# A selective state-space layer with gated experts in fp32: matmuls on zeros at the start, and one exponential moved from VectorE to GpSimd

## The chip, the cores and the metric

The kernel runs on one core of a Trainium2 chip. The metric is the device time of one execution in microseconds (us); the time of a kernel is the median of its runs. A profiled execution gives the span from its first to its last instruction and a trace of what every engine did. The engines are TensorE (PE in the profile, its weight loads PEld), VectorE (DVE), ScalarE (ACT), GpSimd (POOL) and the queues that issue DMAs (SP, and those of ACT and POOL).

## The reference

`x` has 64 sequences (b), 64 heads (h) and 1024 positions (l), all fp32. Each head has a convolution kernel over the positions, made of 64 complex modes, and the result goes through a layer of 64 experts of rank 16, of which each token takes 16:

```python
dt = exp(log_dt);  A = -exp(log_A_real) + 1j * A_imag;  dtA = A * dt[:, None]
Cs = C * (exp(dtA) - 1) / A
K  = 2 * einsum('hn,hnl->hl', Cs, exp(dtA[:, :, None] * arange(L))).real
y  = causal_conv(x * mask, K) + x * mask * D[:, None]      # then * mask; mask = l < length[b]
scores = y @ Wr.T;  gates = softmax of the 16 largest scores, zero elsewhere
h   = einsum('nd,krd->nkr', y, A_experts)
out = x + 2 * einsum('nkr,kdr->nd', h * gates[:, :, None], B_experts)
```

The part that the change touches is `Cs`, the factor of each mode. With dtA = u + iv it needs exp(u) - 1, the sine of v and 1 - cos v, and a division by A. The kernel forms exp(u) itself as s * (1 + q): s is a power of two, q a polynomial of degree eight, so that exp(u) - 1 = s q + (s - 1).

## The kernel before

**Staging.** The heads are worked in 8 groups of 8 heads (512 tokens). For each group, tables of the modes' powers give a Toeplitz block (`toep`) and two factors (`bt`, `w`) of a chunked convolution: TensorE forms the states of each chunk (`pu`, L652), VectorE carries them from chunk to chunk (L664 to L670), and TensorE adds the part inside a chunk (`pc`, L681) and the part across (L690). Then come the scores (L760) and the first expert product (L585), which is a seven-product scheme for 2x2 blocks. The second expert product (L1083) is in the last third of the span and uses a two-level scheme of the same kind.

**The start.** Everything waits for the parameters of the modes. `par_sb` (log dt, log of -A's real part, A's imaginary part, C) is the first load on SP. VectorE forms dt and the real part of A by `exp_parts` (L413) on 128x64, then `dt_re` = u (`p_dtre`, L449) and `theta` = v, and the angle in turns in two parts (`tu_hi`, `tu_lo`; L454 to L464). Then several chains run:

- `tables(0)` (L240), the wide tables of the first group on 128x516: magnitude by ScalarE (L252), angle by VectorE (L253 to L264), sines by ScalarE (L267 to L270), and the two multiplies into `w` (L273, L275);
- `real_part` (L470): a second `exp_parts` on `dt_re`, 128x32, and `em1` = exp(u) - 1;
- `angle` (L477): the sines of the modes' angles, `s2`, and the reciprocal of |A|^2 (`rden`);
- `products` (L515): the factors `alpha`, `beta` and their negatives.

`together` (L401) takes one step of each chain in turn. These instructions are issued on VectorE in the order in which they are written (`first_order`, L435, a manual schedule), and so are ScalarE's up to L551 (`first_copies`). In `products`, `e_im` (L517) is the first that uses `em1`; the first `w` multiply follows it. With `alpha` and the others, VectorE makes `b` (L350 to L354), TensorE turns it (`pb`, L337), ScalarE copies it (`bt`, L339), and `pu` follows.

**The sums of the expert weights.** The seven-product scheme needs sums of quarters of the weight matrix `at`. The quarters arrive on SP (L165). TensorE forms two of the sums by multiplying each addend with the identity into one bank (`factors_by_identity`, L187): four banks, three addends each, 128x512. ScalarE copies the banks out (`s1` at L200, `s2` at L204); the first of these copies is in ScalarE's order before the sines, the other seven after them and before `bt`. GpSimd waits for the last x tile of the group (`behind_landing`, L206) and then issues DMAs that add the other sums (L214, L223).

**The order on TensorE** is set by the planner of the framework, from its own costs and the order of writing, save for instructions named in `keep_in_program_order`, which keep their order among themselves. `ps_c` holds two PSUM banks, used later by `pc`.

Of the kernel before, what the change touches and what calls it, by code (L numbers as in the profile page):

```python
# [37 lines left out]
F32 = mybir.dt.float32  # L38
I32 = mybir.dt.int32
AF = mybir.ActivationFunctionType  # L40
ALU = mybir.AluOpType
# [3 lines left out]
P = 128  # L45
NB = 64
NH = 64
L = 1024
# [14 lines left out]
NP = NH // 2  # L63
# [29 lines left out]
def body(ctx: ExitStack, tc, x, xo, lens, par, dvec, dgrp, at, bm, wt, cst, out):  # L93
    nc = tc.nc
    V = nc.vector
    G = nc.gpsimd
# [4 lines left out]
    def pool(stack, name, bufs, side, **kw):  # L101
        return stack.enter_context(tc.tile_pool(name=name, bufs=bufs, side=side, **kw))
# [4 lines left out]
    ps_c = psum.enter_context(tc.tile_pool(name="ps_c", bufs=2, space=PSUM))  # L107
# [15 lines left out]
    prep = pool(prep_ctx, "prep", 1, "right")  # L123
# [13 lines left out]
    ident = cst_sb[:, NW : NW + P]  # L137
# [16 lines left out]
    def factor(wpool, name, t):  # L154
        return wpool.tile([P, KH, L // 2], F32, tag=t, name=f"{name}{t}")
# [31 lines left out]
    def factors_by_identity(a21, a22, a11, a12, out):  # L187


        s1, s2, s4 = (factor(wp, "wa", t) for t in ("s1", "s2", "s4"))  # L190
        out.extend((a11, a12, s4, a22, s1, s2, a21))
        banks = [ps_f.tile([P, L // 2], F32, tag="pf", name=f"sum_{k}") for k in range(KH)]

        def add(bank, a, first=False, last=False):
            nc.tensor.matmul(bank, lhsT=ident, rhs=a, start=first, stop=last, skip_group_check=True)

        for k in range(KH):
            add(banks[k], a21[:, k, :], first=True)
            add(banks[k], a22[:, k, :])
            nc.scalar.copy(s1[:, k, :], banks[k])  # L200
            yield
        for k in range(KH):
            add(banks[k], a11[:, k, :], last=True)
            nc.scalar.copy(s2[:, k, :], banks[k])  # L204
            yield
# [176 lines left out]
    def new(name, w=NP, dtype=F32, keep=False):  # L382
        pool = const if keep else prep
        return pool.tile([P, w], dtype, tag=f"p_{name}", name=f"p_{name}")

    def tt(o, a, b, o_):
        V.tensor_tensor(out=o, in0=a, in1=b, op=o_)  # L387
        return o

    def ts(o, a, s1, o1, s2=None, o2=None):  # L390
        if o2 is None:
            V.tensor_scalar(out=o, in0=a, scalar1=s1, scalar2=None, op0=o1)
        else:
            V.tensor_scalar(out=o, in0=a, scalar1=s1, scalar2=s2, op0=o1, op1=o2)
        return o

    def stt(o, a, s, o1, b, o2):
        V.scalar_tensor_tensor(out=o, in0=a, scalar=s, in1=b, op0=o1, op1=o2)  # L398
        return o

    def together(*chains):  # L401

        chains = list(chains)
        while chains:
            for c in list(chains):
                if next(c, chains) is chains:
                    chains.remove(c)

    def some(it, n):
        for _ in range(n):  # L410
            yield next(it, None)

    def exp_parts(xin, name, w, out):  # L413

        xc = ts(new(name + "x", w), xin, -87.0, ALU.max, 88.0, ALU.min)
        k = ts(new(name + "k", w), xc, LOG2E, ALU.mult)
        yield
        ts(k, k, MAGIC, ALU.add, MAGIC, ALU.subtract)
        yield
        stt(xc, k, -LN2_HI, ALU.mult, xc, ALU.add)  # L420
        yield
        stt(xc, k, -LN2_LO, ALU.mult, xc, ALU.add)
        s = new(name + "s", w, I32)
        ts(s, k, 127.0, ALU.add, 8388608.0, ALU.mult)
        yield
        q = ts(new(name + "q", w), xc, 1.0 / math.factorial(8), ALU.mult)
        for i in range(7, 0, -1):
            yield
            stt(q, q, 1.0 / math.factorial(i), ALU.add, xc, ALU.mult)
        out += [s.bitcast(F32), q]  # L430
# [5 lines left out]
    first_order.enter_context(tc.manual_schedule(engines={V.engine}))  # L436
    first_copies = ExitStack()
    first_copies.enter_context(tc.manual_schedule(engines={nc.scalar.engine}))
    log_both = par_sb[:, 0:2, :].rearrange("p a h -> p (a h)")
    a_im, c_re, c_im = (par_sb[:, i, :] for i in (2, 3, 4))  # L440
    parts = []
    together(exp_parts(log_both, "e", 2 * NP, parts))
    s, q = parts
    both = new("both", 2 * NP)
# [3 lines left out]
    a_re = ts(new("are"), both[:, NP:], -1.0, ALU.mult)  # L448
    dt_re = tt(new("dtre", keep=True), a_re, dt, ALU.mult)  # L449
    theta = tt(new("theta"), a_im, dt, ALU.mult)  # L450

    hi, lo, t1 = new("hi"), new("lo"), new("t1")
# [14 lines left out]
    parts = []  # L467
    em1, r, sin, s2, den, rden = (new(n) for n in ("em1", "r", "sin", "s2", "den", "rden"))

    def real_part():  # L470
        yield from exp_parts(dt_re, "f", NP, parts)
        yield
        tt(em1, parts[0], parts[1], ALU.mult)
        yield
        stt(em1, parts[0], -1.0, ALU.add, em1, ALU.add)

    def angle():  # L477
        ts(r, turns, MAGIC, ALU.add, MAGIC, ALU.subtract)
        yield
        tt(r, tu_hi, r, ALU.subtract)  # L480
        yield
        tt(r, r, tu_lo, ALU.add)
        yield
        ts(r, r, HALF_IN, ALU.min, -HALF_IN, ALU.max)
        nc.scalar.activation(sin, r, AF.Sin, scale=2.0 * math.pi)
        nc.scalar.activation(s2, r, AF.Sin, scale=math.pi)
        yield
        tt(den, a_re, a_re, ALU.mult)
        yield
        tt(t1, a_im, a_im, ALU.mult)  # L490
        yield
        tt(den, den, t1, ALU.add)
        yield
        V.reciprocal(rden, den)
        yield
        tt(s2, s2, s2, ALU.mult)
        yield
        ts(s2, s2, 2.0, ALU.mult)

    wa, wb = [], []  # L500
    marks = {}
    sums = factors_by_identity(*wa_quarters, wa)
    steps0 = tables(0)
    next(steps0)
    for _ in some(sums, 1):
        pass
    together(some(steps0, 5), real_part(), angle())

    e_im = new("eim")
    e_re = new("ere")  # L510
    n_re, n_im, t2 = new("nre"), new("nim"), new("t2")
    alpha, nbeta, nalpha = (new(n, keep=True) for n in ("alpha", "nbeta", "nalpha"))
    beta = new("beta")

    def products():  # L515
        ts(e_re, s2, -1.0, ALU.mult, 1.0, ALU.add)
        stt(e_im, em1, 1.0, ALU.add, sin, ALU.mult)  # L517
        yield
        tt(e_re, e_re, em1, ALU.mult)
        tt(t1, e_im, a_im, ALU.mult)  # L520
        tt(n_im, e_im, a_re, ALU.mult)
        yield
        tt(e_re, e_re, s2, ALU.subtract)
        yield
        tt(n_re, e_re, a_re, ALU.mult)
        tt(t2, e_re, a_im, ALU.mult)
        yield
        tt(n_re, n_re, t1, ALU.add)
        tt(n_im, n_im, t2, ALU.subtract)
        yield  # L530
        tt(n_re, n_re, rden, ALU.mult)
        tt(n_im, n_im, rden, ALU.mult)
        yield
        tt(alpha, c_re, n_re, ALU.mult)
        tt(t1, c_im, n_im, ALU.mult)
        tt(beta, c_re, n_im, ALU.mult)
        tt(t2, c_im, n_re, ALU.mult)
        yield
        tt(alpha, alpha, t1, ALU.subtract)
        tt(beta, beta, t2, ALU.add)  # L540
        yield
        ts(alpha, alpha, 2.0, ALU.mult)
        ts(nbeta, beta, -2.0, ALU.mult)
        ts(nalpha, alpha, -1.0, ALU.mult)

    together(products(), some(steps0, 2))
    scales.update(alpha=alpha, nbeta=nbeta, nalpha=nalpha)

# [591 lines left out]
    def steps_of(g):  # L1140
        return tables(g) if g < NG else iter(())
# [14 lines left out]
    y = got.pop()  # L1156
    spread = {}
    products, done = counted(first(0, y, spread)), [0]
    ahead(products, 1)
    for _ in steps:  # L1160
        pass
    ahead(products, 1)
    for g in range(NG):
# [18 lines left out]
        if g == 0:  # L1182
            tables1, n = steps_of(1), 0
# [50 lines left out]
    n = 0  # L1234
    for _ in products:
# [3 lines left out]
        if n in (5, 6):  # L1239
            i = (1, 6)[n - 5]  # L1240
# [18 lines left out]
    def lpool(name, bufs):  # L1259
        return pool(ctx, name, bufs, "left")  # L1260

    tp2 = lpool("tp2", 1)
    op = [lpool(f"op{i}", 4) for i in range(3)]
# [55 lines left out]
```

## Time and profile before

| | |
|---|---|
| Time, median of 3 runs | 961.89 us (961.85 to 961.9) |
| Profiled execution | 961.78 us |
| Its span | 960.0 us |
| Mean granted TensorE clock | 1.000 |
| TensorE busy | 948.8 us, 99% of the span |
| VectorE busy | 729.1 us, 76% |
| GpSimd busy | 332.5 us, 35% |
| ScalarE busy | 152.4 us, 16% |

How to read it: the page gives busy time by engine, the chain of work that ended last, and groups of instructions. A line of a group has the source line, the engine, the operation, output and inputs with their shapes and count, then total busy time and the mean in ns, then the idle time of the engine just before them and what ended it. A line of the timeline has the start in us from the span's beginning, the duration in us, the engine, the line and the instruction; in brackets is the idle time before it and what released it. Names in the trace carry a prefix: `p_em` is `em1`, `p_eim` is `e_im`, `was` and `waa` are the quarters and sums of the weights (the tiles' common beginnings), `sum` is one of the four banks.

The start in short: the first instruction of VectorE after `par_sb` has landed is at 3.22 us, the first matmul at 4.14 us, the first `pb` at 19.79 us and the first `pu` at 21.76 us.

### The profile page before, as it was taken

What the parts mean: (1) busy time and instruction counts of PE and PEld (TensorE: products, weight loads), DVE (VectorE), ACT (ScalarE), POOL (GpSimd) and SP (SyncE); (2) the same over time, 40 slices, a digit from 0 to 9 for tenths busy, and PEclk for the clock granted to TensorE, in tenths of its full rate; (3) what the DMA queues carried; (4) which work ended last, traced back from release to release, by engine and by line L of the source; (5) the groups of instructions that cost most, each with busy time, mean ns of one, the idle gap of its engine ahead of it and who ended that gap; (6) DMA issues with size and microseconds to landing.
All of it is one profiled execution on the core that took longest, in us unless ns stands there. A gap on an engine that the chain in (4) does not pass through costs nothing.

```text
span 960.0 us, 11875 instructions
## 1 busy us (share of the span) xinstructions
PE 948.8 (99%) x4259; PEld 723.4 (75%) x4259; DVE 729.1 (76%) x1697; ACT 152.4 (16%) x302; POOL 332.5 (35%) x285
## 2 busy tenths in 40 slices
PE   7999999999999999999999999999999999999998
PEld 2476676676676676676686588888888888888887
DVE  8899899597687687687577589878956875786674
ACT  5345051311410320220101000000000000000000
POOL 0212212051051051051041022248645654854565
PEclk9999999999999999999999999999999999999999
DMA  8916244162262252244341273662683476268332
GB/s 285 231 42 183 100 129 150 45 182 87 91 190 77 88 176 94 88 134 121 102 137 57 78 259 129 247 258 78 219 307 98 165 241 208 77 220 289 116 115 104
DMA packets 68985, 143.97 MB, mean 150 GB/s; under 512 B 9472, under 2 KB 20288, under 8 KB 68928
## 3 DMA queue, kind: packets, MB, share of 16 engines
q1 hardware_dynamic: 49420, 94.40, 29.2%
q0 software_dynamic: 16864, 47.22, 15.6%
q10 hardware_dynamic: 2644, 1.61, 0.6%
q8 instruction: 33, 0.54, 0.2%
q14 instruction: 24, 0.20, 0.1%
HBM read 94.89 MB, written 47.25 MB: 148 GB/s over the span
## 4 chain that ended last, share of the span: by engine, by line
PE 97%; DVE 2%; DMA 0%; issue 0%; ACT 0%; DVEq 0%
PE h L585 41%; PE s L1083 35%; PE pc L681 6%; PE pc L690 5%; PE pu L652 5%; PE psh L760 3%; PE pb L337 1%; PE psc L770 0%; PE last L1083 0%; DMA par_sb<-in_par 0%; DVE ey L918 0%; DVE p_eq L398 0%; DVE y L698 0%; DVE f L387 0%; DVE w L387 0%
## 5 line engine op out<-in xcount | busy, mean ns | idle before, releaser
L398 DVE SCALAR_TENSOR_TENSOR s<-s,turn 128x128 f32<-128x128 f32 (+1 forms) x558 | 154.2, 325 | 21.0 <-ACT s L657 15.6
L585 PE MATMUL h<-y,waa 128*128 128x256 f32 x512 | 119.4, 382 | 0.0
L585 PE MATMUL h<-y,was 128*128 128x256 f32 x512 | 117.1, 381 | 0.0
L585 PE MATMUL h<-ty,was 128*128 128x256 f32 x512 | 116.1, 379 | 0.0
L585 PEld LDWEIGHTS h<-y,waa 128*128 128x128 f32 x512 | 95.1, 190 | 23.9 <-issue 7.6
L585 PEld LDWEIGHTS h<-y,was 128*128 128x128 f32 x512 | 96.2, 190 | 19.1 <-issue 5.7
L585 PEld LDWEIGHTS h<-ty,was 128*128 128x128 f32 x512 | 97.0, 190 | 14.6 <-issue 1.5
L845 POOL TENSOR_TENSOR hg<-h_p,gx 128x512 f32<-128x512 f32 x16 | 27.6, 1727 | 221.2 <-DVE h_p L398 217.2
L845 POOL TENSOR_TENSOR hg<-h_u,gx 128x512 f32<-128x512 f32 x32 | 47.7, 1491 | 100.7 <-DVE h_u L387 96.5
L698 DVE TENSOR_TENSOR y<-pc,mask 128x512 f32<-128x512 f32 x64 | 41.2, 683 | 45.1 <-PE pc L690 45.1
L1097 ACT COPY p<-s 128x512 f32<-128x512 f32 x28 | 16.4, 585 | 312.4 <-PE s L1083 312.4
L942 POOL TENSOR_TENSOR o<-o,acc_a 128x512 f32<-128x512 f32 x32 | 47.7, 1509 | 41.4 <-ACT acc_a L960 21.6
L818 POOL DMA_DIRECT2D gx<-gt_dram x56 | 34.1, 624 | 73.9 <-DMA gt_dram<-gt 73.8
L681 PE MATMUL pc<-x,toep 128*128 128x512 f32 x128 | 58.9, 594 | 0.0
L585 PE MATMUL h<-ty,waa 128*128 128x256 f32 x256 | 58.4, 381 | 0.0
L657 ACT COPY s<-pu 128x448 f32<-128x448 f32 x62 | 32.7, 531 | 157.0 <-PE pu L652 157.0
L585 PEld LDWEIGHTS h<-ty,waa 128*128 128x128 f32 x256 | 48.2, 190 | 9.9 <-issue 3.5
L652 PE MATMUL pu<-x,bt 128*64 128x448 f32 x256 | 53.4, 549 | 0.0
L690 PE MATMUL pc<-s,w 64*128 64x448 f32 x248 | 52.8, 555 | 0.0
L942 POOL TENSOR_TENSOR o<-o,b_room 128x512 f32<-128x512 f32 x32 | 49.1, 1556 | 9.8 <-DVE b_room L387 9.8
L387 DVE TENSOR_TENSOR o<-o,s 128x512 f32<-128x512 f32 x50 | 34.1, 681 | 23.0 <-PE s L1083 17.3
L387 DVE TENSOR_TENSOR hg<-hg 128x512 f32<-128x512 f32 x64 | 43.0, 684 | 9.2 <-POOL hg L845 8.5
(238 smaller groups left out, 1570.1 us busy)
## 6 DMA issues: line engine op xcount, KB each, us to landing
x<-in_x SPq DMA_DIRECT2D x32, 512.0 KB
hg_dram<-hg POOLq DMA_DIRECT2D x16, 1024.0 KB, 5.8
o<-in_xo SPq DMA_DIRECT2D x64, 256.0 KB
out<-o SPq DMA_DIRECT2D x63, 256.0 KB
gx<-gt_dram POOLq DMA_DIRECT2D x56, 256.0 KB, 5.4
qy<-hg_dram SPq DMA_DIRECT2D x28, 512.0 KB
r<-hg_dram SPq DMA_DIRECT2D x26, 512.0 KB
hg_dram<-hg POOLq DMA_DIRECT2D x16, 768.0 KB, 4.9
```

Of the source, the lines that this page charges most:

```text
L387: V.tensor_tensor(out=o, in0=a, in1=b, op=o_)
L398: V.scalar_tensor_tensor(out=o, in0=a, scalar=s, in1=b, op0=o1, op1=o2)
L585: nc.tensor.matmul(bank[:, ii, :], lhsT=fac[n - 1][:, k, (j + ii) * P : (j + ii + 1) * P], rhs=rf[n - 1][:, k, :], start=(first and ii == ...
L652: nc.tensor.matmul(pu[hh * NS : (hh + 1) * NS, :], lhsT=bt[:, i, (1 - c) * P + hh * NS : (1 - c) * P + (hh + 1) * NS], rhs=xt[:, hh, : NCH ...
L657: marks["s"] = nc.scalar.copy(s[:, c], pu.rearrange("p (k b) -> p k b", b=NB))
L681: nc.tensor.matmul(pc, lhsT=toep[:, 2 * i + hh, :], rhs=xt[:, hh, :], start=True, stop=False)
L690: m = nc.tensor.matmul(pcs[hh][:, NB:], lhsT=w[o : o + NS, c, i, 1:], rhs=s[o : o + NS, c].rearrange("p k b -> p (k b)"), start=False, sto ...
L698: marks["y"] = V.tensor_tensor(out=y[:, :, i // 2, 2 * (i % 2) + hh, :], in0=pcs[hh].rearrange("p (k b) -> p k b", b=NB), in1=mask, op=ALU ...
L818: i = queue.dma_start(gx[:, ii, :], gt_dram[g, c * n : (c + 1) * n, :].unsqueeze(1).to_broadcast([n, RANK, TOK]),)
L845: G.tensor_tensor(out=o, in0=a, in1=b, op=op)
L942: tc.keep_in_program_order(G.tensor_tensor(out=o, in0=a, in1=b, op=op_))
L1083: nc.tensor.matmul(bank[:, ii, :], lhsT=left_[i - 1][:, k, ii * P : (ii + 1) * P], rhs=right_[i - 1][:, k, :], start=(first and ii == rows ...
```

## The change

There are three edits.

1. A tile `idle` of 128x512 zeros is set by VectorE ahead of its first other work. TensorE multiplies it with itself: four matmuls of 128x512 ahead of the first sum's first addend, and four after that addend. Their results go to banks of `ps_c` and are not read. They and the first addend keep their order.
2. `exp_parts` takes an engine. `real_part` gives it GpSimd and does its own three steps there too; it is written ahead of the other chains and takes no part in `together` any more. On GpSimd a `scalar_tensor_tensor` is written as a `tensor_scalar` into a tile of its own and a `tensor_tensor`.
3. On VectorE some small steps are merged: the square of `s2` with its factor 2; the factor 2 of `alpha` and `beta` goes into `den` as a factor 0.5; `nbeta` is formed directly with its sign. `e_im` stays where it was.

```diff
--- before.py
+++ after.py
@@ -191,11 +191,23 @@
         out.extend((a11, a12, s4, a22, s1, s2, a21))
         banks = [ps_f.tile([P, L // 2], F32, tag="pf", name=f"sum_{k}") for k in range(KH)]
 
+        def unread(n):
+            for i in range(n):
+                bank = ps_c.tile([P, L // 2], F32, tag="pc", name="unread")
+                tc.keep_in_program_order(
+                    nc.tensor.matmul(bank, lhsT=idle[:, :P], rhs=idle, start=True, stop=True))
+
+        unread(4)
+
         def add(bank, a, first=False, last=False):
-            nc.tensor.matmul(bank, lhsT=ident, rhs=a, start=first, stop=last, skip_group_check=True)
+            return nc.tensor.matmul(bank, lhsT=ident, rhs=a, start=first, stop=last,
+                                    skip_group_check=True)
 
         for k in range(KH):
-            add(banks[k], a21[:, k, :], first=True)
+            i = add(banks[k], a21[:, k, :], first=True)
+            if k == 0:
+                tc.keep_in_program_order(i)
+                unread(4)
             add(banks[k], a22[:, k, :])
             nc.scalar.copy(s1[:, k, :], banks[k])
             yield
@@ -410,7 +422,20 @@
         for _ in range(n):
             yield next(it, None)
 
-    def exp_parts(xin, name, w, out):
+    def exp_parts(xin, name, w, out, E=V):
+
+        def ts(o, a, s1, o1, s2=None, o2=None):
+            two = {} if o2 is None else dict(op1=o2)
+            E.tensor_scalar(out=o, in0=a, scalar1=s1, scalar2=s2, op0=o1, **two)
+            return o
+
+        def stt(o, a, s, o1, b, o2):
+            if E is V:
+                E.scalar_tensor_tensor(out=o, in0=a, scalar=s, in1=b, op0=o1, op1=o2)
+            else:
+                t = ts(new(name + "t", w), a, s, o1)
+                E.tensor_tensor(out=o, in0=t, in1=b, op=o2)
+            return o
 
         xc = ts(new(name + "x", w), xin, -87.0, ALU.max, 88.0, ALU.min)
         k = ts(new(name + "k", w), xc, LOG2E, ALU.mult)
@@ -436,6 +461,8 @@
     first_order.enter_context(tc.manual_schedule(engines={V.engine}))
     first_copies = ExitStack()
     first_copies.enter_context(tc.manual_schedule(engines={nc.scalar.engine}))
+    idle = prep.tile([P, L // 2], F32, tag="idle", name="idle")
+    V.memset(idle, 0.0)
     log_both = par_sb[:, 0:2, :].rearrange("p a h -> p (a h)")
     a_im, c_re, c_im = (par_sb[:, i, :] for i in (2, 3, 4))
     parts = []
@@ -468,11 +495,11 @@
     em1, r, sin, s2, den, rden = (new(n) for n in ("em1", "r", "sin", "s2", "den", "rden"))
 
     def real_part():
-        yield from exp_parts(dt_re, "f", NP, parts)
-        yield
-        tt(em1, parts[0], parts[1], ALU.mult)
-        yield
-        stt(em1, parts[0], -1.0, ALU.add, em1, ALU.add)
+        for _ in exp_parts(dt_re, "f", NP, parts, G):
+            pass
+        G.tensor_tensor(out=em1, in0=parts[0], in1=parts[1], op=ALU.mult)
+        G.tensor_scalar(out=parts[1], in0=parts[0], scalar1=-1.0, scalar2=None, op0=ALU.add)
+        G.tensor_tensor(out=em1, in0=parts[1], in1=em1, op=ALU.add)
 
     def angle():
         ts(r, turns, MAGIC, ALU.add, MAGIC, ALU.subtract)
@@ -485,17 +512,16 @@
         nc.scalar.activation(sin, r, AF.Sin, scale=2.0 * math.pi)
         nc.scalar.activation(s2, r, AF.Sin, scale=math.pi)
         yield
-        tt(den, a_re, a_re, ALU.mult)
-        yield
-        tt(t1, a_im, a_im, ALU.mult)
+
+        stt(den, a_re, 0.5, ALU.mult, a_re, ALU.mult)
+        yield
+        stt(t1, a_im, 0.5, ALU.mult, a_im, ALU.mult)
         yield
         tt(den, den, t1, ALU.add)
         yield
         V.reciprocal(rden, den)
         yield
-        tt(s2, s2, s2, ALU.mult)
-        yield
-        ts(s2, s2, 2.0, ALU.mult)
+        stt(s2, s2, 2.0, ALU.mult, s2, ALU.mult)
 
     wa, wb = [], []
     marks = {}
@@ -504,7 +530,8 @@
     next(steps0)
     for _ in some(sums, 1):
         pass
-    together(some(steps0, 5), real_part(), angle())
+    real_part()
+    together(some(steps0, 5), angle())
 
     e_im = new("eim")
     e_re = new("ere")
@@ -533,14 +560,12 @@
         yield
         tt(alpha, c_re, n_re, ALU.mult)
         tt(t1, c_im, n_im, ALU.mult)
-        tt(beta, c_re, n_im, ALU.mult)
+        stt(beta, c_re, -1.0, ALU.mult, n_im, ALU.mult)
         tt(t2, c_im, n_re, ALU.mult)
         yield
         tt(alpha, alpha, t1, ALU.subtract)
-        tt(beta, beta, t2, ALU.add)
-        yield
-        ts(alpha, alpha, 2.0, ALU.mult)
-        ts(nbeta, beta, -2.0, ALU.mult)
+        tt(nbeta, beta, t2, ALU.subtract)
+        yield
         ts(nalpha, alpha, -1.0, ALU.mult)
 
     together(products(), some(steps0, 2))
```

## The prediction

> **What bounds the kernel now.** I read the page's busy shares first, then the chain that ended last, then the timeline of the first 30 us engine by engine. The page and the chain's shares by engine:
>
> ```profile
> PE 948.8 (99%) x4259; PEld 723.4 (75%) x4259; DVE 729.1 (76%) x1697; ACT 152.4 (16%) x302; POOL 332.5 (35%) x285
> ...
> PE 97%; DVE 2%; DMA 0%; issue 0%; ACT 0%; DVEq 0%
> ```
>
> TensorE is 97% of the chain. The change adds and removes work only ahead of the first `pu` product (L652), so what matters is when that product starts: 21.76 us now. After it the chain is TensorE's own work and I find no wait there for an event fixed in time (the chain's DMA share is the one load of `par_sb`), so a shift of the 21.76 passes on one for one. The timeline of Vector where it sets that start (start, duration, instruction):
>
> ```profile
> 7.21 0.19 DVE L387 TENSOR_TENSOR p_dtre<-p_are,p_both 128x32 f32<-128x32 f32 x1
> ...
> 15.30 0.19 DVE L398 SCALAR_TENSOR_TENSOR p_em<-p_fs,p_em 128x32 f32<-128x32 f32 x1
> ...
> 15.53 0.19 DVE L398 SCALAR_TENSOR_TENSOR p_eim<-p_em,p_sin 128x32 f32<-128x32 f32 x1
> ...
> 16.55 0.69 DVE L387 TENSOR_TENSOR w<-mag,sh 128x516 f32<-128x516 f32 x1
> ...
> 19.00 0.28 DVE L392 TENSOR_SCALAR b<-w,p_alpha 128x128 f32<-128x128 f32 x1
> ...
> 19.79 0.59 PE L337 MATMUL pb<-cst_sb,b 128*128 128x128 f32 x2 [0.75 <-DVE b L398]
> ```
>
> Vector runs without a gap from 3.22 on and TensorE waits for it (0.75 us before `pb`). The value the change moves, `p_em`, is made of `p_dtre` (ready at 7.40) and is wanted at 15.53. From `e_im` to the first `b` it is 19.00 - 15.53 = 3.47 us. TensorE's side of the same stretch:
>
> ```profile
> 4.14 2.04 PE L195 MATMUL sum<-was,cst_sb 128*128 128x512 f32 x2 [4.14 <-DMA was<-in_at]
> 7.59 2.08 PE L195 MATMUL sum<-waa,cst_sb 128*128 128x512 f32 x2 [1.40 <-DMA waa<-in_at]
> ...
> 11.74 1.88 PE L195 MATMUL sum<-was,cst_sb 128*128 128x512 f32 x4
> 13.46 5.58 PE L195 MATMUL sum<-waa,cst_sb 128*128 128x512 f32 x12
> ```
>
> One fp32 matmul of 128x512 is two records. They follow each other at about 0.86 us early and at 0.43 us from about 10.9 us; 24 of them end near 19.04.
>
> **The change, part by part.**
>
> *Vector loses work.* Sixteen small operations of the second exponential go (fourteen of `exp_parts`, two of `em1`); in the chain they take 0.04 to 0.20 us each, together about 2.0 us. Merging `s2` saves one operation, the two scalings in `products` two more: of these the two after `e_im` shorten 3.47 to about 3.26 us (0.1 each). The folded factor 0.5 in `den` and `t1` is free: the scalar form takes the same 0.19 us as the plain one on 128x32. With nothing else in the way `e_im` could start about 1.8 us sooner, near 13.7. The memset of `idle` lies in Vector's empty time before 3.22 (0.42 us, by the 128x516 tensor_scalar row; without that cover 0.42 us).
>
> *GpSimd gets a chain.* It has no fused scalar-tensor form here, so each of nine such steps of `exp_parts` is two instructions: five plain ones plus 2 x 9 make 23, and `em1` three, **26 instructions, each reading the one before or nearly so**. They start at 7.40 + 0.05. So `e_im` can start at 7.5 + 26 p, with p the time of one step with its handoff. The trace shows no 128x32 operation of GpSimd. The two nearest rows:
>
> ```profile
> L208 POOL COPY landed<-x 1x1 f32<-1x1 f32 x1 | 0.4, 445 | 22.6 <-DMA x<-in_x 22.6
> ...
> L942 POOL TENSOR_TENSOR b_room<-acc_a,u 128x512 f32<-128x512 f32 x12 | 15.0, 1265 | 34.2 <-DVE u L387 34.2
> ```
>
> A single element costs 0.445 us, 512 columns 1.265. The line through both gives 0.445 + 31 x 0.0016 = 0.49 us at 32 columns: the upper end, 26 x 0.49 = 12.7. Against it stands the Trainium skill, "GPSIMD Engine Reference", Performance versus the Vector engine: about 2.6 cycles an element at 1.2 GHz for two inputs, 4497 ns at 2048 columns. With the 512-column row that is (4497 - 1265) / 1536 = 2.1 ns a column and a fixed part of 0.19 us, so an estimate of 0.26 us at 32 columns: the lower end, 6.8 us. By the rule `e_im` could start at 14.3, earlier than the 15.53 of now, by the row at 20.2. The two copies of one element agree (445 and 438 ns) and are nearest in size, so I lean to them; but both come straight after a long wait, and half of the steps have one input only, so I take **p = 0.41**: 26 x 0.41 = 10.7 us, `e_im` at 18.15, the first `b` at 18.15 + 3.26 = 21.4 against 19.00: **+2.4 us**. Break-even is p = (19.00 - 3.26 - 7.5) / 26 = 0.317.
>
> The same skill speaks against the idea: "SBUF — State Buffer", SBUF: two separate sides, says that GpSimd and a Vector instruction in a two-port mode or with two SBUF inputs lock one port pair for whole instructions. From 7.5 to 12.7 nearly all of Vector's instructions are of these kinds, up to 0.69 us long. The row fits without proving it: GpSimd's 128x512 products run between 1.26 and 1.74 us. Without a lock p stays in the 0.26 to 0.49 above; if ten of the steps wait 0.2 us each, that is 2 us more, or p = 0.49 from 0.41. This keeps p above the rule's end. The delay of Vector in return lies behind Vector's own wait for `em1`.
>
> GpSimd's queue: the copy behind x's landing (23.51) and the third sum's DMAs (24.15) queue behind these 26. They would be held up only with p above 0.61. Vector's order is written out: behind the waiting `e_im` stand both `w` multiplies, all of `products`, every `b`, and then TensorE.
>
> *TensorE multiplies zeros.* Eight matmuls are 16 records. SP, ACT and POOL begin their own work at 0.74, so the memset ends near 1.15 and TensorE starts at 1.2. The skill's "TensorE: Matmul & The Clock Gate", Part 1, has half rate until one busy window of about 3.4 us. The records agree with half rate (0.86 against 0.43), while the granted clock stands at 1.00 through it; and it took 3.0 us of the second burst, 6.5 from the first. By the page's window 4 records are cold, by the trace's 6.5 us up to 8. All 24 + 16 = 40 records back to back: 1.2 + 40 x 0.43 + (4 to 8) x 0.43 = **20.1 to 21.8** for the end of the sums, against 19.04. So the warm clock gains nothing here: eight extra matmuls cost more (6.9 us) than the idle time and cold time they take. In the likeliest case this hides: `pb` waits for `b` until 22.2, and the last copy of a sum (0.58 us) is done by 22.4, before the first `bt` copy (22.8). Without this cover it is the first rival.
>
> Scalar: the first sum's copy (9.70 now) waits for 20 records, 1.2 + 8.6 + 1.7 to 3.4 = 11.5 to 13.2; the table load (1.28) and the sines move after it, and the last `sh` step ends at 16.1 to 17.8 instead of 15.66. It hides behind the second `w` multiply at 19.2.
>
> *Sum.* Profiled execution 960.0 + 2.4 = 962.4 of span; 1.8 us lie around it (961.78 against 960.0), so **964.2**; by the median of the runs, 961.89 + 2.4, 964.3. I say 964.2.
>
> **Rivals.**
>
> 1. *GpSimd is in time, and TensorE's zeros set the start.* p below 0.317, as the skill's price has it. Then `pu` starts 1.4 us after the sums end (two `pb` of 0.44, `pk` 0.52): 21.5 to 23.2 against 21.76, -0.3 to +1.4; Scalar's chain gives `b` at 18.3 to 20.0, within that. 961.6 to 963.3, centre 962.4: not slower by the bound below. For it: the page's slope, and no wait of GpSimd on itself in the trace. Against: the 0.44 us copies.
>
> 2. *GpSimd is a little late.* p from 0.32 to 0.39: +0.1 to +1.9, 962.0 to 963.8, also within the bound. It turns into my forecast at p = (1.92 + 15.74 - 7.5) / 26 = 0.391.
>
> 3. *The order of later work changes.* TensorE's order outside the pinned instructions is planned, and another order in the first group's stages moves a few us either way. Now the idle time there is small (TensorE 99% busy), so there is little to win: about 959.5 if it helps, 966 if it hurts.
>
> 4. *It does what its words say*: early warm sums and a Vector chain 1.8 us shorter give 960.1. The sum of 40 records speaks against it; it needs both p below 0.27 and the zeros done before 7.59, where (7.59 - 1.2 - 4 x 0.43) / 0.43 = 11 of the 18 records ahead of the second addend fit.
>
> **How the numbers follow.** A measurement tells this kernel from no change by about 0.2%, 1.92 us: faster is below 959.97, slower above 963.81. Forecast (p over 0.391) 0.48; rival 2, 0.20; rival 1, 0.20; rival 3, 0.09, of it 0.04 faster and 0.05 slower; rival 4, 0.03, of which I count 0.02 faster. That gives slower 0.53, same 0.41, faster 0.06. The forecast's own range is 963.8 to 968 (p to 0.55 with the lock). The range over all cases: the low end is rival 1's best, 961.6, the high end p = 0.53, +5.5, 967.4; outside lie rival 4, the good half of rival 3, and the largest p.
>
> **What would show it.** Right: 26 GpSimd instructions between 7.5 and about 18, start to start near 0.41; Vector idle for 4 to 5 us before `p_eim`, released by POOL `p_em`; `pb` waits for `b` of Vector near 22.2; `pu` near 24.2. TensorE with 16 further records and sums ending at 20 to 22. Wrong: `p_eim` at or before 15.7, or its wait put down to ACT; `pb` following the sums without a gap. Also wrong would be a first `pu` at the forecast time and an end that doesn't move with it, which would mean slack later on that I don't see.

## The result and the profile after

The changed kernel takes 966.45 us (median of five runs, 966.15 to 967.29) against 961.85 us before. The ratio is 1.0049, with a 95% interval of 1.0035 to 1.0063: it is slower by 4.6 us. The forecast was 964.2 us, slower by 2.4. The direction and the range (961.6 to 967.4) held; the size was half of what came.

Up to the first `pu` product the forecast is met almost to the tenth. From the timeline of the profiled execution of the changed kernel, Vector and TensorE (start, duration, instruction):

```profile
7.21 0.19 DVE L399 TENSOR_TENSOR p_dtre<-p_are,p_both 128x32 f32<-128x32 f32 x1
...
18.24 0.19 DVE L410 SCALAR_TENSOR_TENSOR p_eim<-p_em,p_sin 128x32 f32<-128x32 f32 x1 [2.45 <-POOL p_em L502]
...
21.50 0.28 DVE L404 TENSOR_SCALAR b<-w,p_alpha 128x128 f32<-128x128 f32 x1
...
22.29 0.59 PE L349 MATMUL pb<-cst_sb,b 128*128 128x128 f32 x2 [0.64 <-DVE b L410]
...
24.26 3.33 PE L677 MATMUL pu<-x,bt 128*64 128x448 f32 x16
```

`e_im` starts at 18.24 us (forecast 18.15) and waits for GpSimd's `em1`; the first `b` follows 3.26 us later, as forecast; `pu` starts at 24.26 (forecast 24.2, before 21.76). That is 2.50 us late.

TensorE's side, the same timeline:

```profile
1.45 6.47 PE L198 MATMUL unread<-idle 128*128 128x512 f32 x8 [1.45 <-DVE idle L465]
7.75 1.02 PE L203 MATMUL sum<-was,cst_sb 128*128 128x512 f32 x2
8.61 3.60 PE L198 MATMUL unread<-idle 128*128 128x512 f32 x8
12.04 1.02 PE L203 MATMUL sum<-waa,cst_sb 128*128 128x512 f32 x2
...
17.20 4.45 PE L203 MATMUL sum<-waa,cst_sb 128*128 128x512 f32 x10
```

The sums end at 21.65 us, within the 20.1 to 21.8 of the forecast, and are hidden behind `b`. But the end of the span is 4.7 us late, not 2.5. The page's chain shows that something other than TensorE now stands in it (shares of the span by engine):

```profile
PE 91%; DVE 4%; DMA 2%; POOL 1%; issue 1%; ACT 1%; POOLq 0%; DVEq 0%
```

TensorE's share was 97% before. Of the missing 2.2 us, 2.0 are two waits of TensorE, at 33 and at 112 us, that were not there before. The groups of the page show them behind the second bar, as the idle time before a group and what ended it; the timeline shows when they fall:

```profile
L610 PE MATMUL h<-y,was 128*128 128x256 f32 x512 | 117.2, 381 | 1.0 <-DVE h_p L410 1.0
...
L706 PE MATMUL pc<-x,toep 128*128 128x512 f32 x128 | 58.9, 594 | 1.1 <-DMA toep<-krows 1.1
...
33.52 3.70 PE L706 MATMUL pc<-x,toep 128*128 128x512 f32 x8 [1.07 <-DMA toep<-krows]
...
112.44 3.72 PE L610 MATMUL h<-y,was 128*128 128x256 f32 x16 [0.96 <-DVE h_p L410]
```

**The first wait** is for the Toeplitz block. SP's timeline of before, a write of the kernel rows to DRAM (2 KB) and the read that makes the block of them; the read is issued once the write has landed:

```profile
22.84 0.31 SPq L325 DMA_DIRECT2D krows<-ks  x1
24.01 0.39 SPq L327 DMA_DIRECT2D toep<-krows  x1
```

and of the changed kernel, with GpSimd's DMAs of the third sum:

```profile
23.77 2.68 POOL L226 DMA_DIRECT2D was<-in_at  x2 [0.23 <-PE pb L349]
...
25.52 0.31 SPq L337 DMA_DIRECT2D krows<-ks  x1
29.06 0.39 SPq L339 DMA_DIRECT2D toep<-krows  x1
```

The write took 1.17 us from issue to the next issue, and now takes 3.54. The third sum's DMAs (24.15 before) stand behind a small copy that waits for x to land; the bracket names `pb`, but that copy ended 0.23 us before them. x landed no later than before (0.4 us earlier), while the rows moved by 2.7 us, from ahead of these DMAs to behind them.

**The second wait** is Vector's order. The planner now has three of the four additions of the first gated product (`hg`) at the head of the recurrence over the chunks of group 1 (`s`): two before its first step and one behind it. They wait for GpSimd, and the recurrence waits with them. Vector's timeline of the changed kernel:

```profile
77.50 0.68 DVE L877 TENSOR_TENSOR hg<-h,gx 128x512 f32<-128x512 f32 x1
82.89 1.42 DVE L399 TENSOR_TENSOR hg<-hg 128x512 f32<-128x512 f32 x2 [4.71 <-POOL hg L870]
84.23 0.34 DVE L410 SCALAR_TENSOR_TENSOR s<-s,turn 128x128 f32<-128x128 f32 x1
```

and before, where the recurrence (33 steps from 77.14) ran in that time:

```profile
74.12 0.68 DVE L852 TENSOR_TENSOR hg<-h,gx 128x512 f32<-128x512 f32 x1
75.74 0.87 DVE L398 SCALAR_TENSOR_TENSOR s<-s,turn 128x128 f32<-128x128 f32 x3 [0.94 <-ACT s L657]
```

Later work on Vector is late by what it idled there, among it `h_p`, for which TensorE waits 0.96 us near 112 us. TensorE's own order did not change: its 429 matmul records from the first `pu` to the scores of group 1 come in the same sequence in both traces.

### The profile page after: what moved, and what is told of

The parts are those of the page before. It is cut to its first block, busy times and chain, and to the rows that moved or that the text cites. A ratio compares the mean times of both kernels' runs of the same rounds, so it can differ in the third digit from the quotient of the medians.

```text
span 964.7 us, 11915 instructions
## 1 busy us (share of the span) xinstructions
PE 955.6 (99%) x4275; PEld 726.9 (75%) x4275; DVE 725.0 (75%) x1679; ACT 152.6 (16%) x302; POOL 341.7 (35%) x311
## 4 chain that ended last, share of the span: by engine, by line
PE 91%; DVE 4%; DMA 2%; POOL 1%; issue 1%; ACT 1%; POOLq 0%; DVEq 0%
PE h L610 37%; PE s L1108 34%; PE pc L706 5%; PE pc L715 5%; PE pu L677 4%; PE psh L785 3%; DVE s L410 2%; PE pb L349 1%; DMA gx<-gt_dram 1%; DMA toep<-krows 0%; DMA krows<-ks 0%; PE psc L795 0%; PE last L1108 0%; POOL p_ft L429 0%; DVE w L399 0%
## 5 line engine op out<-in xcount | busy, mean ns | idle before, releaser
L410 DVE SCALAR_TENSOR_TENSOR s<-s,turn 128x128 f32<-128x128 f32 (+1 forms) x558 | 151.2, 321 | 21.5 <-ACT s L682 16.3
```

## The experiments

The theory after the result: the late `em1` costs 2.5 us, and the other 2.1 us are these two waits, which the lateness brings with it. Rivals: the zeros cost part of it; GpSimd's steps disturb something else; the two waits are one. Eleven further kernels were run. This table is read from the profiled executions of ten of them (the eleventh, vector_quiet, is a measurement of GpSimd's steps alone): the start of the first `pu`; the start of the scores of group 1 (`psh`, 119.66 us before); how much longer than before it takes from the one to the other (97.90 us before); and from there to the end of the span.

| kernel | time, median us | ratio, 95% interval | `pu` | `psh` | between, over before | `psh` to the end |
|---|---|---|---|---|---|---|
| before | 961.85 | | 21.76 | 119.66 | | 840.3 |
| changed | 966.45 | 1.0035 to 1.0063 | 24.26 | 124.27 | +2.11 | 840.4 |
| no_zeros | 967.04 | 1.0043 to 1.0068 | 24.59 | 126.45 | +3.96 | 840.4 |
| no_gpsimd | 962.68 | 0.9999 to 1.0015 | 22.54 | 120.48 | +0.04 | 840.4 |
| merges_only | 961.71 | 0.9988 to 1.0005 | 21.56 | 119.44 | -0.02 | 840.4 |
| third_sum_late | 965.27 | 1.0023 to 1.0048 | 24.19 | 123.74 | +1.65 | 840.4 |
| sums_after_recur | 964.71 | 1.0018 to 1.0041 | 23.96 | 122.53 | +0.67 | 840.4 |
| both_mended | 964.13 | 1.0015 to 1.0032 | 24.07 | 121.96 | -0.01 | 840.4 |
| short_series_zeros | 960.38 | 0.9976 to 0.9989 | 20.38 | 118.27 | -0.01 | 840.4 |
| short_series | 961.09 | 0.9983 to 1.0000 | 20.79 | 118.68 | -0.01 | 840.3 |
| delay_alone | 966.71 | 1.0033 to 1.0063 | 24.76 | 123.82 | +1.16 | 840.4 |
| three_zeros | 961.58 | 0.9985 to 1.0002 | 21.36 | 119.25 | -0.01 | 840.4 |

The last column is the same in all rows within 0.1 us: everything is decided in the first 124 us, and what is lost there reaches the end one for one.

**Which part of the change: no_zeros, no_gpsimd, merges_only.** The first takes out the zeros:

```diff
-        unread(4)
...
-            i = add(banks[k], a21[:, k, :], first=True)
-            if k == 0:
-                tc.keep_in_program_order(i)
-                unread(4)
+            add(banks[k], a21[:, k, :], first=True)
...
-    V.memset(idle, 0.0)
```

> The changed kernel without the matmuls on zeros and without the tile of zeros; the exponential stays on GpSimd and the merged steps stay. If GpSimd's chain sets the start (my account), the zeros were hidden: e_im stays at 18.2 us, the first pu product at 24.2 to 24.3, and the time stays within 0.3 us of the changed kernel, 966.2 to 966.8. If the zeros cost part of the loss, pu comes earlier and the time falls by their share, up to 966.45 - 1.4 = 965.

The second puts the exponential back on Vector and keeps the zeros:

```diff
     def real_part():
-        for _ in exp_parts(dt_re, "f", NP, parts, G):
-            pass
-        G.tensor_tensor(out=em1, in0=parts[0], in1=parts[1], op=ALU.mult)
...
+        yield from exp_parts(dt_re, "f", NP, parts)
+        yield
+        tt(em1, parts[0], parts[1], ALU.mult)
...
-    real_part()
-    together(some(steps0, 5), angle())
+    together(some(steps0, 5), real_part(), angle())
```

> The changed kernel with the exponential back on Vector, in turn with the other chains as before; zeros and merged steps stay. My account: Vector no longer waits, so the zeros show: the sums end at 21.6 as in the changed kernel, the copies of the sums follow, and pu starts near 23.0 instead of 21.76, so 1.2 to 2.0 us slower than before, 963.1 to 963.9. The rival that the zeros do what they say (an earlier warm clock) gives 961.9 or less.

The third does both, so that only Vector's merged steps are left of the change:

> Neither zeros nor GpSimd: only the merged small steps on Vector. My account: three operations of about 0.1 us fewer on the chain ahead of b, pu at 21.4 to 21.6, 961.5 to 961.7. If Vector's chain did not set the start, 961.85, no change.

Without GpSimd nearly all of the loss goes (962.68 us). What is left, 0.8 us, is less than expected: `pu` at 22.54 instead of 23.0, because TensorE's records reached full rate earlier in that execution (at 5.9 us; 7.3 in the changed kernel's) and the sums ended at 21.06. The interval just reaches no change. Without both, 961.71 us can't be told from before, though `pu` came 0.2 us earlier, as expected.

Without the zeros I had expected no effect on the time. The medians (967.04 and 966.45) do not tell the two kernels apart, since their intervals overlap. But the trace shows an effect that I had not expected. The timeline of TensorE in no_zeros (its profiled execution, 968.6 us, is the longest of five):

```profile
14.15 5.31 PE L195 MATMUL sum<-waa,cst_sb 128*128 128x512 f32 x12
22.06 0.74 PE L338 MATMUL pb<-cst_sb,b 128*128 128x128 f32 x2 [2.60 <-DVE b L399]
...
24.59 5.30 PE L664 MATMUL pu<-x,bt 128*64 128x448 f32 x16
...
114.62 3.72 PE L597 MATMUL h<-y,was 128*128 128x256 f32 x16 [0.96 <-DVE h_p L399]
```

and stretches of the same execution (stretch, length, busy time of PE, PEld, DVE, ACT and POOL, granted clock, DMA):

```profile
20.00:22.00 2.00, 0.00 (x0) 0.00 (x0) 2.00 (x17) 0.09 (x1) 0.00 (x0) 1.00 0.75 287
22.00:24.00 2.00, 1.76 (x5) 0.81 (x6) 2.00 (x10) 0.62 (x2) 0.29 (x1) 0.50 0.09 33
24.00:26.00 2.00, 2.00 (x6) 0.53 (x6) 1.87 (x10) 0.49 (x2) 1.77 (x2) 0.50 0.00 0
```

The sums end at 19.46, TensorE idles for 2.60 us, and the granted clock falls to half: the first sixteen `pu` records take 5.30 us instead of 3.33. In the changed kernel the zeros keep TensorE busy until 21.65 and the clock stays up; its mean over the execution is 1.000 in all five runs of the changed kernel and 0.996 to 0.998 in all five of no_zeros. So the zeros were not merely hidden: beside the late exponential they saved the cold clock's cost (2.0 us in `pu` in this execution). What they saved of the whole time is not settled: 2.1 us between the two profiles, 0.6 us between the medians. Part of the cold clock's cost comes back, since no_zeros has no wait for the Toeplitz block (TensorE comes to it later, and the rows' write took 1.2 us); the wait for `h_p` is there as in the changed kernel.

**The first wait: third_sum_late.** The third sum's DMAs move behind the landing of the Toeplitz block:

```diff
-    behind_landing(x_tiles[6][0:1, 1, 0:1])
-    third_sum(wa_quarters[0])
...
             behind_landing(toep[0:1, HG - 1, 0:1])
+            third_sum(wa_quarters[0])
             fourth_sum(wa[2], wa[5])
```

> The changed kernel, but the two DMAs of the third sum are issued behind the landing of the Toeplitz block, ahead of the fourth sum's, instead of behind the landing of x. My account of 0.8 us of the loss: those DMAs start at a time that x sets (23.8) and now run beside the write and the read of the Toeplitz rows, which came 2.7 us later; without them the rows' write lands in about 1.2 us as before instead of 3.5, TensorE's wait of 1.07 us for the block goes, pc starts at 32.4 instead of 33.5, and the time falls by 0.8 to 1.1 us to 965.3 to 965.7. If the block is late for another reason, the wait stays and the time with it.

965.27 us. SP's timeline of this kernel:

```profile
25.26 0.31 SPq L337 DMA_DIRECT2D krows<-ks  x1
26.44 0.39 SPq L339 DMA_DIRECT2D toep<-krows  x1
29.76 0.25 SPq L337 DMA_DIRECT2D krows<-ks  x1
30.97 0.36 SPq L339 DMA_DIRECT2D toep<-krows  x1
```

Both writes now land in 1.2 us and TensorE's wait for the block is gone (`pc` at 32.31). So it was these DMAs. The median falls by 1.2 us, a little more than expected. In the profile, though, which is the longest of its five executions, only 0.46 of the 2.11 us goes: at 112 us TensorE still waits 0.96 us for `h_p`, and at 91.7 it waits 0.37 us for the recurrence (`s`), as it did not in the changed kernel.

**The second wait, and both: sums_after_recur, both_mended.** The additions are held behind the recurrence:

```diff
             def sums():
+                with ExitStack() as held:
+                    if (g, j) == (0, 0):
+                        held.enter_context(tc.issue_after(marks["recur"][1].ins))
...
+                    marks["recur"] = g, V.scalar_tensor_tensor(
```

> The changed kernel with one order set by hand: Vector's four additions of the first gated product (hg sums of group 0) are held behind the recurrence over chunk pairs 0 and 1 of group 1, which is how the planner placed them before the change; in the changed kernel it placed three of them ahead and Vector waited 4.71 us there for GpSimd. My account: TensorE's wait of 0.96 us for h_p near 111 us goes and the time falls by 0.8 to 1.1 us, 965.3 to 965.7. If that order is harmless, TensorE's wait and the time stay (966.2 to 966.8).

> The changed kernel with the third sum's DMAs behind the landing of the Toeplitz block and with the hand-set order of Vector's additions. If the loss is one late start of 2.4 to 2.5 us plus these two, the two add up and what is left is the late start alone: pu at 24.2, no wait of TensorE for the block or for h_p, 964.2 to 964.6. If the two are one cause, it stays with third_sum_late at 965.2.

The order alone takes off 1.7 us by the medians (964.71), more than expected: 1.44 us after `pu`, the rest from an earlier start of this execution. What is left after `pu`, 0.67 us, goes with the DMAs. Both together give 964.13 us, just under the expected range, with nothing left between `pu` and `psh`: just the late start, and 964.2 was the forecast for just the late start. The two waits have two causes, but what each is worth alone does not add up: 1.2 and 1.7 us by the medians, 2.3 together. In the profile of third_sum_late TensorE starts `pc` 1.2 us earlier than in the changed kernel, but Vector's held additions only 0.5 us earlier (82.35 against 82.89), because the last of GpSimd's DMAs that fetch the gates (`gx`) landed only 0.5 us earlier; so TensorE waits for Vector's recurrence instead.

**Is it GpSimd or the lateness: delay_alone.** The kernel before, with a delay on Vector and nothing else (it multiplies `em1` by one):

```diff
         ts(e_re, s2, -1.0, ALU.mult, 1.0, ALU.add)
+        for _ in range(12):
+            ts(em1, em1, 1.0, ALU.mult)
```

> The kernel before with nothing of the change but a delay: twelve small dependent Vector instructions (em1 times one, 128x32) ahead of e_im, 12 x 0.21 = 2.5 us. No GpSimd, no zeros, no merged steps; the order of Vector's later additions stays as before. If lateness alone is what costs, pu starts near 24.3, and since TensorE then has nothing from 19.0 to about 22.3, its clock falls as in no_zeros and the first pu products take 5.3 instead of 3.3 us: 2.5 + 1 to 2, so 965.0 to 966.4. If the warm clock survives the gap, 964.3 to 965.

966.71 us, 0.3 above the expected range and not to be told from the changed kernel. There the additions keep their old order and no wait for `h_p` appears; the clock falls instead. TensorE's and SP's timelines:

```profile
22.36 0.59 PE L337 MATMUL pb<-cst_sb,b 128*128 128x128 f32 x2 [2.07 <-DVE b L398]
23.28 0.60 PE L337 MATMUL pb<-cst_sb,b 128*128 128x128 f32 x2 [0.33 <-DVE b L398]
23.81 1.01 PE L297 MATMUL pk<-b,cst_sb 128*2 128x256 f32 x2
24.76 4.49 PE L654 MATMUL pu<-x,bt 128*64 128x448 f32 x16
...
25.44 0.31 SPq L325 DMA_DIRECT2D krows<-ks  x1
29.02 0.39 SPq L327 DMA_DIRECT2D toep<-krows  x1
```

So lateness of `em1` suffices for a loss of this size, but the loss is made of other parts: `pu` starts 3.00 us late (`pb` 2.57; the rest is `pk` at the fallen clock) and takes 1.16 us longer. The rows' write takes 3.58 us here too, beside the third sum's DMAs (issued at 23.26), so lateness does bring the slow write of the first wait; only TensorE, slowed, comes after the block has landed. The second wait is not shown to come from lateness. The planner's new order stands in all four kernels here that have the exponential on GpSimd and no order set by hand (the changed one, no_zeros, third_sum_late, vector_quiet), and in none of the seven that have it on Vector, of which delay_alone is as late as the changed kernel. So it goes with the move to GpSimd as it is planned, not with when `em1` is ready on the chip; why the planner's costs turn out so is open.

**What one GpSimd step costs: vector_quiet.** GpSimd's chain runs while Vector is held:

```diff
+    real_part()
     hi, lo, t1 = new("hi"), new("lo"), new("t1")
+    V.tensor_copy(hi, em1)
...
-    real_part()
     together(some(steps0, 5), angle())
```

> A measurement, not a version: the changed kernel with GpSimd's 26 steps moved ahead of Vector's angle and table work, and a small copy of em1 on Vector that holds Vector until they are done. In the changed kernel the first 13 steps, beside Vector's work, took 5.84 us (0.45 each), the last 13, with Vector idle, 4.62 (0.36 each). If Vector's instructions hold GpSimd up, all 26 now take 0.36, 9.2 to 9.4 us from the first to the end of em1, and no step stands out at 0.57 to 0.64. If the first steps are slow by their kind, the chain stays at 10.7 us. The time itself is 7 to 11 us longer than before, since Vector's work follows in place of lying beside.

The groups of GpSimd in the changed kernel (busy time, mean ns, idle time before):

```profile
L429 POOL TENSOR_SCALAR p_ft<-p_fq 128x32 f32<-128x32 f32 x7 | 2.4, 340 | 0.6
L437 POOL TENSOR_TENSOR p_fq<-p_ft,p_fx 128x32 f32<-128x32 f32 x7 | 1.9, 277 | 0.6
L437 POOL TENSOR_TENSOR p_fx<-p_ft,p_fx 128x32 f32<-128x32 f32 x2 | 1.2, 581 | 0.2
```

and with Vector quiet:

```profile
L429 POOL TENSOR_SCALAR p_ft<-p_fq 128x32 f32<-128x32 f32 x7 | 2.0, 288 | 0.6
L437 POOL TENSOR_TENSOR p_fq<-p_ft,p_fx 128x32 f32<-128x32 f32 x7 | 1.8, 252 | 0.6
L437 POOL TENSOR_TENSOR p_fx<-p_ft,p_fx 128x32 f32<-128x32 f32 x2 | 0.5, 250 | 0.2
```

The chain takes 9.24 us (7.40 to 16.64) instead of 10.7, 0.355 us a step. The same instruction takes 250 ns alone and 581 beside Vector's wide tables. (Its one run, 972.03 us, is no version: Vector's work follows instead of lying beside.) So what Vector does meanwhile costs the chain 1.5 us. In the changed kernel the two slow `p_fx` steps end at 10.00 and 11.19, each 0.1 us after a 128x516 Vector instruction of two inputs that lay beside it (ends at 9.89 and 11.09), as if they had waited for it.

**How many zeros, and a better version: three_zeros, short_series_zeros, short_series.** Three matmuls ahead of the first sum and none behind it, the exponential on Vector:

```diff
-        unread(4)
+        unread(3)
...
                 tc.keep_in_program_order(i)
-                unread(4)
```

> The merged steps and three matmuls on zeros ahead of the first sum, none after; the exponential on Vector as before. It tells whether no_gpsimd's loss is the zeros as such or their number. By number: six records fit into the idle time before 7.6, the sums end near 17.5 instead of 21.1, Vector bounds the start again at 21.4 to 21.5: 961.4 to 961.7, 0.9 to 1.3 us less than no_gpsimd. If zeros as such cost, it stays above 962.3.

961.58 us. TensorE's timeline:

```profile
1.46 4.27 PE L198 MATMUL unread<-idle 128*128 128x512 f32 x6 [1.46 <-DVE idle L464]
5.57 1.02 PE L203 MATMUL sum<-was,cst_sb 128*128 128x512 f32 x2
7.72 1.12 PE L203 MATMUL sum<-waa,cst_sb 128*128 128x512 f32 x2 [1.13 <-DMA waa<-in_at]
```

The zeros end before the second addend lands (it waits for its DMA again), the sums end at 18.85 (later than the expected 17.5), and Vector bounds the start, with `pu` at 21.36. So their number was what cost in no_gpsimd. The last pair shortens Vector's chain:

```diff
     def real_part():
-        yield from exp_parts(dt_re, "f", NP, parts)
...
+        ts(em1, dt_re, 1.0 / math.factorial(5), ALU.mult)
+        for i in range(4, 0, -1):
+            yield
+            stt(em1, em1, 1.0 / math.factorial(i), ALU.add, dt_re, ALU.mult)
```

> On Vector, with the merged steps: exp(u) - 1 by its series to the fifth power, five instructions in place of sixteen; it leaves out the clamp and the splitting by powers of two, so it serves only small u, as here. Three matmuls on zeros ahead of the first sum, none after it. Vector then gives b near 17.4 instead of 19.0; the zeros fit into TensorE's idle time before 7.6, the sums run warm and end near 17.7, and Scalar's last copy of a sum (near 19.05) comes last: pu at 19.9 to 20.3, 960.0 to 960.6. If x's landing bounds it[...], pu stays near 21 and the time at 961.2 or more.

> The same series on Vector with the merged steps and no zeros. If the cold sums are the next bound (in merges_only pb follows the sums without a gap), they end near 19.9 as there and pu stays at 21.4 to 21.6, 961.5 to 961.8: the shorter chain gains nothing without the zeros. If the clock of the sums doesn't matter, it is as fast as short_series_zeros.

With three zeros: 960.38 us, ratio 0.9983 (0.9976 to 0.9989), the only version here that is clearly faster than the kernel before, at the price of serving small exponents only. `pu` starts at 20.38, a little above the expected 19.9 to 20.3, behind Vector's second `b` and not x:

```profile
18.56 0.45 PE L348 MATMUL pb<-cst_sb,b 128*128 128x128 f32 x2
19.33 0.59 PE L348 MATMUL pb<-cst_sb,b 128*128 128x128 f32 x2 [0.33 <-DVE b L409]
```

Without zeros it took 961.09 us, where I had expected no gain at all. Its sums ended at 19.32, not 19.9: the moment at which TensorE's records reach full rate differs from one execution to the next (10.9 us in the profile of before, 13.7 in delay_alone, whose sums start alike). So in that execution the zeros were worth 0.4 us of `pu`; by the medians, 0.7 us.

## Why the prediction was right, and where its size was off

- **What bounds the start** (Vector's chain, then `pu`): right. The step that failed is that behind `pu` there is "no wait there for an event fixed in time", so that a shift passes on one for one: 2.50 us became 4.6. There was no such wait before, but there was an event fixed in time close by: the third sum's DMAs behind x, which the late rows fell behind (a wait of 1.07 us). The other wait (0.96 us) is the planner's new order, which was no matter of the shift at all. A chain without a wait does not show how near the next one is. In both_mended, without these DMAs and with the old order, the shift does pass one for one. The last sign of being wrong on the list was an end that moves less than `pu`; it moved more.
- **26 steps at p = 0.41**: right, 0.413 measured ((18.24 - 7.50) / 26), but that it is right to one part in a hundred is luck. It was chosen between two estimates, and the parts of p were not as I had them. The estimate from the Trainium skill's "GPSIMD Engine Reference" (Performance versus the Vector engine), 0.26 us, is right for the instruction itself (250 ns with two inputs, Vector quiet), the line through the trace's rows, 0.49, was too high. What the estimate lacked is the handoff from one step to the next, 0.08 us, and Vector's presence, (10.7 - 9.24) / 26 = 0.06 us on average, which I had put on top of 0.41. These two, not the copies of one element, are why the chain came late; the handoff alone, 0.355 us a step, is over the break-even of 0.317. Vector's idle time of "4 to 5 us" was 2.45 us for `em1` and 1.66 us before it for ScalarE's sine.
- **The port pair that GpSimd and Vector lock** (the skill's "SBUF — State Buffer", SBUF: two separate sides): I put up to 2 us on it. The runs show 1.5 us for all that Vector does beside the chain. The two `p_fx` steps look as a wait for a two-input instruction would; no run here isolates the port. The row of 1.26 to 1.74 us that I brought for it was no proof.
- **The zeros**: their cost (sums to 21.65) and their cover were right, and so was their price without it, -0.3 to +1.4 us (0.8 in no_gpsimd). "The warm clock gains nothing here" was right for the sums and wrong for what follows: with `b` late it keeps the clock up for `pu`.
- **Vector's order**: this was the third rival, at 0.05 for a loss. It came, not in TensorE's order where I looked for it, and which stayed the same, but in Vector's. The forecast and this rival are not exclusive, and I added up chances where I should have added up costs.
- **The merged steps**: 0.2 us of `pu`, as worked out, too little to measure at the end.

## What to carry to other kernels

When a step on the critical path moves to a slower engine, count its dependent instructions and give each its handoff and what the other engines' work beside it adds, not its duration alone. When a shift is worked out, list what does not shift with it: a transfer that starts on another event, a planner that may reorder, an idle engine whose clock falls. Fill an idle engine only up to the moment its real work arrives (three zeros against eight), and look whether a gap comes later in which its clock would fall.

## What the runs showed of the hardware

- TensorE's clock fell to half (granted clock 0.50) within the 2.60 us without work in no_zeros. In delay_alone the `pb` records after a gap of 2.07 us were still at full rate, and the clock fell 1.3 us after that gap (0.81 from 23.6 to 23.8 us, then 0.50), among short matmuls. The Trainium skill's "TensorE: Matmul & The Clock Gate", Part 1, speaks of an idle window of about 3.4 us; in no_zeros less was enough. Early in every execution the records run at half rate (0.86 us apart) while the granted clock reads 1.00: there only the records tell.
- A write of 2 KB to DRAM took 1.2 us (once 1.6) from its issue to that of the read behind it, and 2.6 to 5.3 us beside the third sum's DMAs when the first of these had been issued 1.75 us or more earlier and they had not landed. Issued 1.0 us after the first of them (no_zeros), it still took 1.2.
- A GpSimd instruction on 128x32 takes 0.25 us with two inputs and 0.22 to 0.34 with one (mostly 0.29), each about 0.08 us after the one it depends on, and up to 0.64 us beside Vector's wide instructions.
